# Values of the first attention as weights-stationary products, stored and turned by VectorE

## The chip, the core and the metric

The kernel runs on one core of one Trainium2 chip. The core has a matrix engine (TensorE, PE in the profile; its weight loads are listed as PEld), a vector engine (VectorE, DVE), an activation engine (ScalarE, ACT), a general engine (GpSimd, POOL), a queue engine (SyncE, SP) that issues nearly all transfers here, and 16 DMA engines. SBUF is the on-chip working memory with 128 partitions; PSUM is the accumulator memory that TensorE writes. The metric is device time in microseconds, the median of the runs.

## The reference

Two layers of gated cross attention and feed-forward over 8 batches of 128 tokens with 512 features. The change is in the first attention (32 heads of 128, 512-feature context):

```python
h_q = (x @ w_q.T).reshape(b, lq, H, DH)
h_k = (key_value_states @ w_k.T).reshape(b, lk, H, DH)
h_v = (key_value_states @ w_v.T).reshape(b, lk, H, DH)
score = jnp.einsum('bqhd,bkhd->bhqk', h_q, h_k) + position_bias[None]
score = softmax(where(mask, score, -inf))
attn = jnp.einsum('bhqk,bkhd->bqhd', score, h_v).reshape(b, lq, H * DH)
out = attn @ w_out.T
```

Then come a 4-bit-weight feed-forward, a second attention with one head of 512 features whose keys are also a projection of the context, and a feed-forward with routed low-rank parts. Everything is float32; products that need the precision are made from a high and a low part of each operand, three matmuls for one.

## The kernel before

**Three stages.** First the keys and queries of all heads are made and stored to DRAM (to about 300 us in the trace). Then come 64 attention units, about 7 us each (to about 770 us). The last stage runs the two feed-forwards and the second attention. A *unit* `u` is one head and one half of the batch (4 batches); a *pair* `p` is two heads, so four units; a *quad* `g` is four heads.

**Projections by seven products.** `seven` makes a 2 x 2 block product with seven block products instead of eight (Winograd's form): left blocks are the weights (`left_parts` builds the seven sums, `split` makes the high part on ScalarE and the low part on GpSimd or VectorE), right blocks are seven prepared sums of the context (`of_context`), kept in SBUF. It is a generator: one step, one block product. ScalarE copies four results out of PSUM, VectorE adds three.

For keys and queries (`tokens=None`) the weights are the stationary operand, and 512 columns of the context (4 batches x 128 tokens) move: the result has the head's features on the partitions and tokens along the row. One block product is 2 x 3 matmuls. For values (`tokens=jj`) it is the other way round: 128 tokens of the context are stationary and 256 weight columns (two heads) move, so that the result has tokens on the partitions, as the attention needs. One block product is 2 token blocks x 2 x 3 = 12 matmuls. `value_steps(g, jj)` makes a quad's values for half of each token range; `all_values` runs through eight quads, and a ninth that is not values but the second attention's keys (`wk1`). `quad_parts` makes the weight parts of the next quad while the present one is used. `make_values(n)` advances this work to step `n`; a unit asks for about 1.74 steps, 126 in all.

**A unit** (`unit(u)`): output projection for two batches of an earlier pair (`project_out`, six matmuls of 512 columns each and one VectorE add), value steps, `attend(u - 4)` (four matmuls of probabilities and values), then `add_masks(u)` on GpSimd and `scores(u)`: four score matmuls, add and maximum on VectorE, `transpose_probs(u - 3)` on VectorE, exponentials on ScalarE, reciprocal on VectorE, scaling on GpSimd.

**The probabilities' way round.** They have to be turned. VectorE transposes only blocks of 32 x 32, so blocks are moved first: `store_probs(u)` stores 256 KB to DRAM (`through`), `move_probs(u - 1)` reads them back by four transfers of 64 KB, 32 partitions each (`moved`), and `transpose_probs` turns them with one instruction over 128 x 512 elements.

**Order of the work.** The framework's scheduler orders the instructions of the units on each engine by its own estimate; in the first and last stage TensorE's order is that of the program. Each engine runs its instructions in order. `behind("name")` puts an instruction after the last one marked with that name on the same engine. SyncE runs its transfers in order too: per unit `through`, four `moved`, the fetches of one unit's queries and keys (`fetch`, two of 256 KB, three units ahead), and a load of weights (`load_wo`, `load_quad`). The transfers take turns at eight completion semaphores.

**Buffers.** `page` holds 14 buffers of 8 KB a partition (context parts, value weight parts, attention results), `v` 15 of 2 KB (values), `raw` 7. PSUM banks: `mm` 3 (value products and output projection), `sc` 2 (scores and one value product), `av` 3.

Of the kernel before, what the change touches and what calls it, by code (L numbers as in the profile page):

```python
# [17 lines left out]
P = 128  # L18
# [21 lines left out]
OUT_LAG = 6  # L40
FIRST = 6
SHORT = 12
QUAD = 4
AHEAD = 3
WARMING = 7


def pipeline(starts):
# [18 lines left out]
def kernel(  # L67
# [143 lines left out]
        put("P3", a12)  # L211
        yield

    def seven(name, left, right, kept, done, tokens=None):


        shape = [P, HALF * P] if tokens is None else [P, 2, N]

        def times(out, which, start, stop):
            w, t = left[which], right[RIGHT[which]]  # L220
            if tokens is None:
                terms = [
                    (
                        (w[:, 0, bass.ts(dc, P)], w[:, 1, bass.ts(dc, P)]),
                        (t[:, 0, dc, :], t[:, 1, dc, :]),
                    )
                    for dc in range(HK)
                ]
                product(out, terms, start, stop, skip_group_check=True)
                return  # L230
            for j in range(2):
                cols = bass.ts(2 * tokens + j, P)
                terms = [
                    (
                        (t[:, 0, dc, cols], t[:, 1, dc, cols]),
                        (w[:, 0, bass.ts(dc, N)], w[:, 1, bass.ts(dc, N)]),
                    )
                    for dc in range(HK)
                ]

                product(out[:, j, :], terms, start and j == 0, stop, skip_group_check=True)

        c1 = ptile(shape, "mm", f"c1_{name}")
        times(c1, "P1", True, False)
        c11 = kept(0, 0)
        mark("copy", nc.scalar.copy(c11, c1))
        yield
        c3 = ptile(shape, "av", f"c3_{name}")
        times(c3, "P5", True, False)
        yield  # L250
        times(c1, "P6", False, False)
        c12 = kept(0, 1)
        mark("copy", nc.scalar.copy(c12, c1))  # L253
        yield
        c2 = ptile(shape, "sc", f"c2_{name}")
        times(c2, "P2", True, True)
        mark("add", nc.vector.tensor_tensor(c11, c2, c11, ALU.add))
        done(0, 0, c11)
        yield
        times(c1, "P7", False, False)  # L260
        c22 = kept(1, 1)
        mark("copy", nc.scalar.copy(c22, c1))
        mark("add", nc.vector.tensor_tensor(c22, c3, c22, ALU.add))
        done(1, 1, c22)
        yield
        times(c1, "P4", False, True)
        c21 = kept(1, 0)
        mark("copy", nc.scalar.copy(c21, c1))
        done(1, 0, c21)
        yield  # L270
        times(c3, "P3", False, True)
        nc.vector.tensor_tensor(c12, c3, c12, ALU.add)
        done(0, 1, c12)
        yield

# [11 lines left out]

    def load_pair(kind, p):
        if p < NP:
            w = {"wk": wk, "wq": wq}[kind]  # L290
            for h in (2 * p, 2 * p + 1):
                load(f"{kind}_{h}", w[:, h])
# [22 lines left out]
                nc.vector.tensor_tensor(sums["P3"], sums["P2"], sums["P6"], ALU.subtract)  # L315
            yield

    def load_quad(g, rows=(0, 1)):

        for i in rows:  # L320
            for j in range(2):
                if g < H // 4:
                    load(f"wv{i}{j}_{g}", wv[:, 2 * g + i, 2 * j : 2 * j + 2])
                else:
                    src = wk1[:, 2 * j : 2 * j + 2, i * N : (i + 1) * N]
                    load(f"wv{i}{j}_{g}", src, (P, 2, N))

    quads = {}

    def quad_parts(g):  # L330

        blocks = [raws.pop(f"wv{i}{j}_{g}") for i in range(2) for j in range(2)]
        if g == H // 4:
            for n, t in enumerate(blocks):
                factor = fnw_p[:, n % 2 * 2 : n % 2 * 2 + 2].unsqueeze(2).to_broadcast([P, 2, N])
                nc.gpsimd.tensor_tensor(t, t, factor, ALU.mult)
            blocks = [t.rearrange("p a n -> p (a n)") for t in blocks]
        more = wide_row("raw", f"more_wv{g}")
        parts = quads[g] = {}
        pages = []  # L340

        def put(which, src):
            if len(parts) % 2 == 0:
                pages.append(page([P, 2, 2, D], f"wv{which}_{g}"))
            t = pages[-1][:, len(parts) % 2]
            by_vector = g < 2 and len(parts) % 2
            split(t[:, 0], t[:, 1], src, nc.vector if by_vector else nc.gpsimd)
            parts[which] = t

        yield from left_parts(*blocks, more, nc.vector if g < 2 else nc.gpsimd, put)  # L350

    wos = {}

# [296 lines left out]
            )  # L650
        nc.vector.tensor_reduce(anykey, mask_u8, AX.X, ALU.max)

    values_of, attns, probs = {}, {}, {}

    def value_steps(g, jj):

        def kept(n, half):
            return slot([P, 2, N], "v", f"v{n}{half}{jj}_{g}")  # L660

        def done(n, half, t):
            values_of[2 * g + n, half, jj] = t

        return seven(f"v{g}{jj}", quads[g], of_context, kept, done, jj)

    def where(u):

# [58 lines left out]

    def move_probs(u):
        moved = slot([P, NQ, HALF, Q32], "moved", f"moved_{u}")
        blocks = probs[u].rearrange("(i q) n f -> n q i f", q=Q32)  # L730
        for j in range(NQ):
            move = nc.sync.dma_start(
                out=moved[bass.ts(j, Q32)].rearrange("p i b k -> p i (b k)"), in_=blocks[j]
            )
        mark("moved", move)
        probs[u] = moved

    def transpose_probs(u):

        t = slot([P, HALF, P], "pT", f"pT_{u}")  # L740
        nc.vector.transpose(by_block(t), probs[u])
        probs[u] = t

    def attend(u):
        h, half = where(u)
        p, i = divmod(h, 2)
        pT = probs.pop(u)
# [4 lines left out]
        cols = bass.ts(i, P)  # L752
        av = ptile([P, HALF, P], "av", f"av_{u}")
        for b in range(HALF):
            v = values_of[p, half, b // 2][:, b % 2, :]
            nc.tensor.matmul(av[:, b, :], lhsT=v[:, cols], rhs=pT[:, b, :], start=True, stop=True)  # L756
        mark("a", nc.scalar.copy(ah, av))  # L757
        mark("al", nc.vector.tensor_tensor(al, av, wide(ah), ALU.subtract))  # L758

# [193 lines left out]
    def keys_and_queries():  # L953
        nonlocal left, sums, before
        for n, (kind, p) in enumerate(order[:-1]):
# [18 lines left out]
            for i, which in enumerate((now, now, before, now, before, now, now)):  # L974
                next(which, None)
                next(casts, None)
                if n == BEFORE // 2 and i == 3:

                    with later():
                        rows.append(next(of_rows))  # L980
                if i == 0:
                    if n + 2 < len(order):
                        load_pair("w" + order[n + 2][0][0], order[n + 2][1])
                    else:
                        load_quad(0)
            before = now
            with behind("add"):
                sums = sums_of(n + 2)
# [12 lines left out]
        parts = quad_parts(0)  # L1001
        for _ in range(2):
            next(parts)
        for u in range(FIRST):
            fetch(u)
# [8 lines left out]


    def all_values():
        for g in range(H // 4 + 1):
            more = g < H // 4
            if g == 0:
                load_quad(1)  # L1020
            yield from value_steps(g, 0)
            following = quad_parts(g + 1) if more else iter(())
            for n, _ in enumerate(value_steps(g, 1)):

                if n % 2 or n == 6:
                    next(following, None)
                    next(following, None)
                yield

    value_work = all_values()  # L1030
    made = 0
# [7 lines left out]
    def loads(u):  # L1039

        p, r = divmod(u, 4)

        n = {1: FIRST}.get(u, u + 3)
        if n > FIRST or u == 1:
            fetch(n)
        if u % 8 in (QUAD, QUAD + 1) and (u - QUAD) // 8 + 2 <= H // 4:
            load_quad((u - QUAD) // 8 + 2, (u % 8 - QUAD,))
# [142 lines left out]
    def keys(b):  # L1190
        half, j = divmod(b, HALF)
        k = work(b, "k", "v")
        for n in range(2):
            cols = bass.ts(n, N)
            with behind("al", "x"):
                nc.vector.scalar_tensor_tensor(
                    k[:, cols],
                    values_of[NP + n, half, j // 2][:, j % 2, :],
                    rcs[:, b : b + 1],
                    bk[:, cols],  # L1200
                    ALU.mult,
# [205 lines left out]
    def ending():  # L1407
# [7 lines left out]
        with behind("exp"):  # L1415
            split_wo(H - 1)
        move_probs(NU - 1)
        with behind("moved"):
            for i in range(2):
                w_ffn.extend(load_page(f"wf{i}", ffn_kept[i]))  # L1420
# [108 lines left out]
```

## Time and profile before

| | |
|---|---|
| median of 3 runs | 908.32 us (908.06 to 908.65) |
| the profiled execution, first to last instruction | 907.1 us |
| DMA traffic | 174.99 MB, mean 193 GB/s |
| issues of `moved` / `through` / `raw_wv` | 256 of 64 KB / 64 of 256 KB / 32 of 256 KB |
| median to landing | 3.0 us / 2.6 us / 4.9 us |
| granted TensorE clock | 1.000 |

The profile's page lists busy time of each engine, groups of instructions with their mean duration and the idle time before them, and DMA issues. Matmuls are pipelined, so the duration of one is longer than its share of the engine; the step from one start to the next is its price. A "stretch" row gives, for a part of the span: its limits and length, then busy us (and instructions) of PE, PEld, DVE, ACT and POOL, the granted clock, the busy share of the DMA engines, and GB/s. SyncE's rows are marked SPq: its time is issuing and waiting, none of it counted as busy.

### The profile page before, as it was taken

The numbers are of one execution on the slowest core, as the hardware profiler recorded it, in microseconds if no ns is written. First come the engines' busy times: TensorE is split into PE (matmuls) and PEld (weight loads), VectorE is DVE, ScalarE is ACT, GpSimd is POOL, SyncE is SP. The second block draws the span as 40 slices with busy tenths as digits, with TensorE's granted clock in tenths as the row PEclk, the third lists the DMA queues.
The fourth block names the chain that finished last, engine by engine and source line by source line (L and its number), as shares of the span: only waits on it lengthen the run. The fifth ranks groups of instructions, "written<-read, shape, count | busy, mean of one in ns | idle before, by whom it ended". The sixth has DMA issues, their size and how long they took to land.

```text
span 907.1 us, 16427 instructions
## 1 busy us (share of the span) xinstructions
PE 900.8 (99%) x5381; PEld 799.2 (88%) x5381; DVE 673.1 (74%) x1353; ACT 503.0 (55%) x1426; POOL 460.3 (51%) x513
## 2 busy tenths in 40 slices
PE   9999999999999999999999999999999999999998
PEld 7888888888888899999999999999999998888897
DVE  7888878789889866777677667666686877565587
ACT  6666555667555545545536445453454544588862
POOL 2355534114322436756747657583866844265441
PEclk9999999999999999999999999999999999999999
DMA  7755477889875956667574765766767566814001
GB/s 256 255 162 163 152 205 232 294 280 285 275 238 204 298 196 186 182 193 221 163 238 151 203 215 153 222 176 201 215 165 208 180 178 177 306 47 143 1 24 71
DMA packets 125223, 174.99 MB, mean 193 GB/s; under 512 B 17105, under 2 KB 54737, under 8 KB 124113
## 3 DMA queue, kind: packets, MB, share of 16 engines
q1 hardware_dynamic: 124992, 173.68, 61.5%
q8 instruction: 42, 0.69, 0.3%
q14 instruction: 45, 0.36, 0.1%
q10 hardware_dynamic: 144, 0.26, 0.1%
HBM read 109.86 MB, written 64.03 MB: 192 GB/s over the span
## 4 chain that ended last, share of the span: by engine, by line
PE 93%; DVE 3%; DMA 2%; ACT 1%; issue 0%; POOL 0%; SPq 0%; DVEq 0%; ACTq 0%; POOLq 0%
PE c_v L178 7%; PE c_v L179 6%; PE c_v L182 6%; PE pso L182 6%; PE pso L178 6%; PE pso L179 6%; PE sc L692 6%; PE av L756 6%; PE c_q L178 6%; PE c_q L179 6%; PE c_q L182 6%; PE c_k L178 4%; PE c_k L179 4%; PE c_k L182 4%; PE tph L1127 1%; DMA cxraw<-in_cxT_dram 1%
## 5 line engine op out<-in xcount | busy, mean ns | idle before, releaser
L709 ACT ACTIVATE s<-s,nm 128x128 f32<-128x128 f32 x256 | 99.8, 392 | 78.8 <-DVE nm L699 54.8
L777 DVE SCALAR_TENSOR_TENSOR x<-pso,tg,x 128x512 f32<-128x512 f32 x128 | 93.4, 741 | 52.2 <-PE pso L182 51.3
L717 POOL TENSOR_TENSOR s<-s,rs 128x512 f32<-128x512 f32 x64 | 66.7, 1042 | 111.1 <-DVE rs L715 63.2
L178 PE MATMUL pso<-wo_h,a 128*128 128x512 f32 x256 | 101.9, 411 | 0.0
L179 PE MATMUL pso<-wo_l,a 128*128 128x512 f32 x256 | 101.5, 397 | 0.0
L182 PE MATMUL pso<-wo_h,a 128*128 128x512 f32 x256 | 101.0, 395 | 0.1
L178 PE MATMUL c_v<-wvP,cxT 128*128 128x256 f32 x288 | 84.8, 294 | 0.2 <-ACT v L253 0.2
L182 PE MATMUL c_v<-wvP,cxT 128*128 128x256 f32 x288 | 81.4, 283 | 0.0
L179 PE MATMUL c_v<-wvP,cxT 128*128 128x256 f32 x288 | 81.4, 283 | 0.0
L757 ACT CAST a<-av 128x512 fp32r<-128x512 f32 x64 | 37.4, 584 | 74.4 <-PE av L756 74.0
L679 POOL TENSOR_TENSOR s<-mneg,bias 128x512 f32<-128x512 bf16 x64 | 75.9, 1186 | 0.1
L756 PE MATMUL av<-pT,v 128*128 128x128 f32 x512 | 71.2, 274 | 0.0
L756 PEld LDWEIGHTS av<-pT,v 128*128 128x128 f32 x512 | 67.1, 191 | 2.8
L692 PE MATMUL sc<-k,q 128*128 128x128 f32 x464 | 65.8, 274 | 0.0
L692 PEld LDWEIGHTS sc<-k,q 128*128 128x128 f32 x464 | 61.9, 191 | 3.2
L178 PE MATMUL c_v<-wvP,cxB 128*128 128x256 f32 x216 | 62.1, 289 | 0.0
L758 DVE TENSOR_TENSOR a<-av,a 128x512 fp32r<-128x512 f32 x64 | 43.4, 679 | 24.9 <-ACT a L757 24.5
L179 PE MATMUL c_v<-wvP,cxB 128*128 128x256 f32 x216 | 61.2, 283 | 0.0
L182 PE MATMUL c_v<-wvP,cxB 128*128 128x256 f32 x216 | 61.1, 283 | 0.0
L170 POOL TENSOR_TENSOR wo_l<-raw_wo,wo_h 128x512 fp32r<-128x512 f32 x32 | 41.4, 1293 | 33.8 <-ACT wo_h L169 33.8
L182 PEld LDWEIGHTS pso<-wo_h,a 128*128 128x128 f32 x256 | 48.2, 188 | 10.8 <-DVE a L758 1.3
L695 DVE TENSOR_TENSOR s<-sc,s 128x512 f32<-128x512 f32 x64 | 43.7, 683 | 17.1 <-PE sc L692 12.4
(277 smaller groups left out, 2808.4 us busy)
## 6 DMA issues: line engine op xcount, KB each, us to landing
keys<-keys SPq DMA_DIRECT2D x64, 256.0 KB, 3.5
queries<-queries SPq DMA_DIRECT2D x64, 256.0 KB, 3.5
through<-s SPq DMA_DIRECT2D x64, 256.0 KB, 2.6
moved<-through SPq DMA_DIRECT2D x256, 64.0 KB, 3.0
q<-queries SPq DMA_DIRECT2D x58, 256.0 KB, 3.8
k<-keys SPq DMA_DIRECT2D x58, 256.0 KB, 4.3
raw_wq<-in_wq_dram SPq DMA_DIRECT2D x32, 256.0 KB, 3.9
raw_wv<-in_wv_dram SPq DMA_DIRECT2D x32, 256.0 KB, 4.9
```

The source lines that it names most:

```text
L170: mark("low", (low_engine or nc.vector).tensor_tensor(low, src, wide(high), ALU.subtract))
L178: nc.tensor.matmul(out, lhsT=lh, rhs=rh, start=first, stop=False, **more)
L179: nc.tensor.matmul(out, lhsT=lh, rhs=rl, start=False, stop=False, **more)
L182: nc.tensor.matmul(out, lhsT=ll, rhs=rh, start=False, stop=last, **more),
L679: nc.gpsimd.tensor_tensor(s, mneg[:, half], bias.unsqueeze(2).to_broadcast([P, NQ, HALF, Q32]), ALU.add)
L692: nc.tensor.matmul(ps[:, j, :], lhsT=q[:, cols], rhs=k[:, cols], start=True, stop=True)
L695: nc.vector.tensor_tensor(s, by_block(ps), s, ALU.add)
L709: e = nc.scalar.activation(one, one, AF.Exp, bias=nm[:, j : j + 1], accum_out=sm[:, j : j + 1])
L717: mark(f"norm{u}", nc.gpsimd.tensor_tensor(s, s, factors, ALU.mult))
L756: nc.tensor.matmul(av[:, b, :], lhsT=v[:, cols], rhs=pT[:, b, :], start=True, stop=True)
L758: mark("al", nc.vector.tensor_tensor(al, av, wide(ah), ALU.subtract))
L777: "x", nc.vector.scalar_tensor_tensor(xs[b], ps, factor, xs[b], ALU.mult, ALU.add, **out)
```

## The change

Values are made as keys are: a pair's weights are stationary, 512 columns of context move, one block product is six matmuls of 512 columns. The result has features on the partitions, so it is stored to DRAM (ordered by 32-token blocks while it is copied out of PSUM, through `view`), read back by four transfers of 32 partitions each, and turned by one VectorE transpose a unit, right after the probabilities' own. The weight parts are made a pair at a time (seven of 256 columns), the first four pairs half on VectorE. The ninth quad, the second attention's keys, is made as before, under new names.

```diff
-    def seven(name, left, right, kept, done, tokens=None):
+    def seven(name, left, right, kept, done, tokens=None, view=lambda t: t):
...
-        mark("copy", nc.scalar.copy(c11, c1))
+        mark("copy", nc.scalar.copy(c11, view(c1)))
...
-        mark("add", nc.vector.tensor_tensor(c11, c2, c11, ALU.add))
+        mark("add", nc.vector.tensor_tensor(c11, view(c2), c11, ALU.add))
...
+    def value_weights(p):
+
+        rows = [raws.pop(f"wv_{h}") for h in (2 * p, 2 * p + 1)]
+        more = slot([P, HK, P], "raw", f"more_wv{p}")
+        a11, a12, a21, a22 = (t[:, :, bass.ts(i, P)] for i in range(2) for t in rows)
+        parts = value_parts[p] = {}
+        pages = []
+        engine = nc.vector if p < BY_VECTOR else nc.gpsimd
+
+        def put(which, src):
+            n = len(parts)
+            if n % 4 == 0:
+                pages.append(page([P, 4, 2, HK, P], f"wv{which}_{p}"))
+            t = pages[-1][:, n % 4]
+            split(t[:, 0], t[:, 1], src, nc.vector if p < BY_VECTOR and n % 2 else nc.gpsimd)
+            parts[which] = t.rearrange("p a dc n -> p a (dc n)")
+
+        yield from left_parts(a11, a12, a21, a22, more, engine, put)
...
-    def value_steps(g, jj):
+    def value_steps(p):
+
+        def kept(i, half):
+            return slot([P, NQ, HALF, Q32], "v", f"v{i}{half}_{p}")
+
+        def done(i, half, t):
+            stored_v = dram.tile([P, NQ, HALF * Q32], F32, tag="values", name=f"values_{p}{i}{half}", bufs=VALUES)
+            with behind("load"):
+                nc.sync.dma_start(out=stored_v, in_=t.rearrange("p n b k -> p n (b k)"))
+            values_of[4 * p + 2 * half + i] = stored_v
+
+        def view(t):
+            return by_block(t.rearrange("p (b k) -> p b k", b=HALF))
+
+        return seven(f"v{p}", value_parts[p], of_context, kept, done, view=view)
...
+    def turn(name, src, moved):
+
+        blocks = src.rearrange("(i q) n f -> n q i f", q=Q32)
+        for j in range(NQ):
+            move = nc.sync.dma_start(
+                out=moved[bass.ts(j, Q32)].rearrange("p i b k -> p i (b k)"), in_=blocks[j]
+            )
+        mark(name, move)
+
+    def move_values(u):
+        if 0 <= u < NU:
+            t = slot([P, NQ, HALF, Q32], "v", f"vmoved_{u}")
+            turn("values", values_of[u], t)
+            values_of[u] = t
+
+    def transpose_values(u):
+        t = slot([P, HALF, P], "v", f"vT_{u}")
+        nc.vector.transpose(by_block(t), values_of[u])
+        values_of[u] = t
...
     def transpose_probs(u):
...
         probs[u] = t
+        transpose_values(u)
...
-            v = values_of[p, half, b // 2][:, b % 2, :]
-            nc.tensor.matmul(av[:, b, :], lhsT=v[:, cols], rhs=pT[:, b, :], start=True, stop=True)
+            nc.tensor.matmul(
+                av[:, b, :], lhsT=v[:, b, :], rhs=pT[:, b, :], start=True, stop=True
+            )
...
     def all_values():
+        load_pair("wv", 2)
+        for p in range(NP):
+            following = value_weights(p + 1) if p + 1 < NP else last_weights()
+            for _ in value_steps(p):
+                next(following, None)
                 yield
+            run(following)
+        for jj in range(2):
+            yield from last_steps(jj)
...
         p, r = divmod(u, 4)
 
+        move_values(u - 2)
         n = {1: FIRST}.get(u, u + 3)
...
         move_probs(NU - 1)
+        move_values(NU - 1)
         with behind("moved"):
```

The new constants are `BY_VECTOR = 4` (pairs whose weight parts are half VectorE's) and `VALUES = 14` (buffers in DRAM for stored values). `loads(u + 1)` is called in unit `u`, so `move_values(u - 2)` there reads the values of unit `u - 1`, after the probabilities of the same unit.

More of the change, by code (lines that the diff above doesn't have):

```diff
@@ L42 @@
 SHORT = 12
-QUAD = 4
 AHEAD = 3
 WARMING = 7
+BY_VECTOR = 4
+VALUES = 14
 def pipeline(starts):
@@ L252, in seven @@
         c12 = kept(0, 1)
-        mark("copy", nc.scalar.copy(c12, c1))
+        mark("copy", nc.scalar.copy(c12, view(c1)))
         yield
@@ L261, in seven @@
         c22 = kept(1, 1)
-        mark("copy", nc.scalar.copy(c22, c1))
-        mark("add", nc.vector.tensor_tensor(c22, c3, c22, ALU.add))
+        mark("copy", nc.scalar.copy(c22, view(c1)))
+        mark("add", nc.vector.tensor_tensor(c22, view(c3), c22, ALU.add))
         done(1, 1, c22)
@@ L267, in seven @@
         c21 = kept(1, 0)
-        mark("copy", nc.scalar.copy(c21, c1))
+        mark("copy", nc.scalar.copy(c21, view(c1)))
         done(1, 0, c21)
@@ L271, in seven @@
         times(c3, "P3", False, True)
-        nc.vector.tensor_tensor(c12, c3, c12, ALU.add)
+        nc.vector.tensor_tensor(c12, view(c3), c12, ALU.add)
         done(0, 1, c12)
@@ L289, in load_pair @@
         if p < NP:
+            if kind == "wv":
+                for i in range(2):
+                    load(f"wv_{2 * p + i}", wv[:, p, 2 * i : 2 * i + 2], (P, 2, N))
+                return
             w = {"wk": wk, "wq": wq}[kind]
@@ L316, in pair_parts, with load_last, last_weights @@
             yield
-    def load_quad(g, rows=(0, 1)):
-        for i in rows:
-            for j in range(2):
[L322 to L339, printed above, removed]
+    value_parts = {}
+    def value_weights(p):
[13 more added lines that the diff above has]
+        yield from left_parts(a11, a12, a21, a22, more, engine, put)
+    def load_last():
+        for i in range(2):
+            for j in range(2):
+                src = wk1[:, 2 * j : 2 * j + 2, i * N : (i + 1) * N]
+                load(f"wk1{i}{j}", src, (P, 2, N))
+    def last_weights():
+        blocks = [raws.pop(f"wk1{i}{j}") for i in range(2) for j in range(2)]
+        for n, t in enumerate(blocks):
+            factor = fnw_p[:, n % 2 * 2 : n % 2 * 2 + 2].unsqueeze(2).to_broadcast([P, 2, N])
+            nc.gpsimd.tensor_tensor(t, t, factor, ALU.mult)
+        blocks = [t.rearrange("p a n -> p (a n)") for t in blocks]
+        more = wide_row("raw", "more_wk1")
+        parts = value_parts[NP] = {}
         pages = []
@@ L343, in put @@
             if len(parts) % 2 == 0:
-                pages.append(page([P, 2, 2, D], f"wv{which}_{g}"))
+                pages.append(page([P, 2, 2, D], f"wk1{which}"))
             t = pages[-1][:, len(parts) % 2]
-            by_vector = g < 2 and len(parts) % 2
-            split(t[:, 0], t[:, 1], src, nc.vector if by_vector else nc.gpsimd)
+            split(t[:, 0], t[:, 1], src, nc.gpsimd)
             parts[which] = t
-        yield from left_parts(*blocks, more, nc.vector if g < 2 else nc.gpsimd, put)
+        yield from left_parts(*blocks, more, nc.gpsimd, put)
     wos = {}
@@ L651, in prep_mask, with last_steps @@
         nc.vector.tensor_reduce(anykey, mask_u8, AX.X, ALU.max)
-    values_of, attns, probs = {}, {}, {}
-    def value_steps(g, jj):
+    values_of, last_of, attns, probs = {}, {}, {}, {}
+    def value_steps(p):
[9 more added lines that the diff above has]
+        return seven(f"v{p}", value_parts[p], of_context, kept, done, view=view)
+    def last_steps(jj):
         def kept(n, half):
-            return slot([P, 2, N], "v", f"v{n}{half}{jj}_{g}")
+            return slot([P, 2, N], "v", f"k1{n}{half}{jj}")
         def done(n, half, t):
-            values_of[2 * g + n, half, jj] = t
-        return seven(f"v{g}{jj}", quads[g], of_context, kept, done, jj)
+            last_of[n, half, jj] = t
+        return seven(f"k1{jj}", value_parts[NP], of_context, kept, done, jj)
+    def turn(name, src, moved):
[14 more added lines that the diff above has]
+        values_of[u] = t
     def where(u):
@@ L729, in move_probs @@
         moved = slot([P, NQ, HALF, Q32], "moved", f"moved_{u}")
[L730 to L735, printed above, removed]
+        turn("moved", probs[u], moved)
         probs[u] = moved
@@ L746, in attend @@
         p, i = divmod(h, 2)
-        pT = probs.pop(u)
+        pT, v = probs.pop(u), values_of.pop(u)
         if i == 0:
@@ L751, in attend @@
         ah, al = a[:, 0], a[:, 1]
-        cols = bass.ts(i, P)
         av = ptile([P, HALF, P], "av", f"av_{u}")
         for b in range(HALF):
-            v = values_of[p, half, b // 2][:, b % 2, :]
-            nc.tensor.matmul(av[:, b, :], lhsT=v[:, cols], rhs=pT[:, b, :], start=True, stop=True)
+            nc.tensor.matmul(
+                av[:, b, :], lhsT=v[:, b, :], rhs=pT[:, b, :], start=True, stop=True
+            )
         mark("a", nc.scalar.copy(ah, av))
@@ L984, in keys_and_queries @@
                     else:
-                        load_quad(0)
+                        load_pair("wv", 0)
+                        load_pair("wv", 1)
             before = now
@@ L1000, in keys_and_queries @@
                     next(extra, None)
-        parts = quad_parts(0)
-        for _ in range(2):
+        parts = value_weights(0)
+        for _ in range(3):
             next(parts)
@@ L1016, in all_values @@
     def all_values():
[L1017 to L1027, printed above, removed]
+        load_pair("wv", 2)
[3 more added lines that the diff above has]
+                next(following, None)
                 yield
+            run(following)
+        for jj in range(2):
+            yield from last_steps(jj)
     value_work = all_values()
@@ L1045, in loads @@
             fetch(n)
-        if u % 8 in (QUAD, QUAD + 1) and (u - QUAD) // 8 + 2 <= H // 4:
-            load_quad((u - QUAD) // 8 + 2, (u % 8 - QUAD,))
+        q = {2: 3}.get(u, p + 3 if p and r == 0 else NP + 1)
+        if q < NP:
+            load_pair("wv", q)
+        elif q == NP:
+            load_last()
         if r == 1:
@@ L1197, in keys @@
                     k[:, cols],
-                    values_of[NP + n, half, j // 2][:, j % 2, :],
+                    last_of[n, half, j // 2][:, j % 2, :],
                     rcs[:, b : b + 1],
```

## The prediction

> **What bounds the kernel now.** I read four views in this order: the page's busy times, the stretches, the PE timeline, and SyncE's queue.
>
> ```profile
> span 907.1 us, 16427 instructions
> PE 900.8 (99%) x5381; PEld 799.2 (88%) x5381; DVE 673.1 (74%) x1353; ACT 503.0 (55%) x1426; POOL 460.3 (51%) x513
> ```
>
> The stretch of the attention units, where all the value products lie but the first and last few (PE, PEld, DVE, ACT, POOL busy, granted clock, DMA share, GB/s):
>
> ```profile
> 350.00:750.00 400.00, 400.00 (x2785) 371.14 (x2784) 281.53 (x498) 197.47 (x652) 261.82 (x226) 1.00 0.66 194
> ```
>
> PE has no idle time there, at full clock. No other engine passes 70%, and the DMA engines are 66% busy. The 58 stores of probabilities in that stretch make 58 units, 6.90 us each. So a shorter PE stream shortens the kernel, as long as nothing else reaches 6.9 us a unit.
>
> Busy means overlap, so the price of a matmul is read from start to start (start, duration, name):
>
> ```profile
> 201.20 0.39 PE L179 MATMUL c_q<-xqT,wqP 128*128 128x512 f32 x1
> 201.43 0.39 PE L182 MATMUL c_q<-xqT,wqP 128*128 128x512 f32 x1
> 201.65 0.39 PE L178 MATMUL c_q<-xqB,wqP 128*128 128x512 f32 x1
> ```
>
> ```profile
> 503.14 0.28 PE L178 MATMUL c_v<-wvP,cxB 128*128 128x256 f32 x1
> 503.26 0.28 PE L179 MATMUL c_v<-wvP,cxB 128*128 128x256 f32 x1
> 503.38 0.28 PE L182 MATMUL c_v<-wvP,cxB 128*128 128x256 f32 x1
> ```
>
> 512 columns cost 0.2265 us (median step of the query products), 256 columns 0.120 us.
>
> SyncE issues nearly every transfer. Its queue in a dense stretch, the stretch's shares, and the waits in that queue (total, times, longest):
>
> ```profile
> 508.10 0.38 SPq L725 DMA_DIRECT2D through<-s  x1
> 508.58 1.92 SPq L732 DMA_DIRECT2D moved<-through  x4
> 510.94 0.34 SPq L615 DMA_DIRECT2D q<-queries  x1
> 511.75 0.34 SPq L615 DMA_DIRECT2D k<-keys  x1
> 512.52 0.33 SPq L285 DMA_DIRECT2D raw_wo<-in_wo_dram  x1
> 513.26 0.32 SPq L725 DMA_DIRECT2D through<-s  x1
> ```
>
> ```profile
> 508.10:513.30 5.20, 5.20 (x35) 4.69 (x34) 4.53 (x9) 3.11 (x14) 1.67 (x2) 1.00 0.94 251
> ```
>
> ```profile
> SPq L725 <- POOL s L717: 112.0, 38, 5.8
> SPq L564 <- DVE keys L272: 29.3, 11, 3.0
> SPq L615 <- DMA k<-keys: 8.1, 15, 1.0
> ```
>
> Eight transfers took 5.2 us here, at 94% of the DMA engines: when SyncE has work it is already short of room. The program uses eight completion semaphores in turn, so an issue waits for the transfer issued eight before; the last of these rows is that wait. Today its spare time is the 112 us spent waiting for the next normalized probabilities.
>
> **The change part by part.**
>
> *Matmuls.* A quad of heads took 2 x 7 products x 2 tokens x 2 x 3 = 168 matmuls of 256 columns; eight quads, 1344. A pair now takes 7 x 2 x 3 = 42 of 512; sixteen pairs, 672. The multiply work is equal; the gain is 672 x (2 x 0.120 - 0.2265) = 9.1 us, all on the path. The last quad (second layer's keys) stays.
>
> The Trainium skill ("TensorE: Matmul & The Clock Gate", Back-to-back issue gap) speaks against even this: it gives 262 and 518 cycles, 109 and 216 ns at the full clock, so a pair of halves would lose only 2.5 ns and the change would save 672 x 2.5 ns = 1.7 us. The rows above show 13.5 ns, and they decide.
>
> *Turning.* 64 more VectorE transposes at the row of the existing ones: 64 x 0.702 = 44.9 us. VectorE goes in the stretch from 281.5 to about 281.5 + 58 x 0.70 = 322 us of 400, 81%. It was at 92% (45.98 of 50 us) at 250 to 300 us with PE full, so I cost this at nothing beside PE. Without cover it is the 44.9 us.
>
> *Splitting the weights.* 112 splits of 256 columns replace 56 of 512. ScalarE: 112 x 0.409 - 56 x 0.620 = +11 us. GpSimd, by these rows:
>
> ```profile
> L170 POOL TENSOR_TENSOR wvP<-raw_wv,wvP 128x512 fp32r<-128x512 f32 x41 | 54.0, 1329 | 2.8 <-ACT wvP L169 2.7
> L170 POOL TENSOR_TENSOR wkP<-raw_wk,wkP 128x256 fp32r<-128x256 f32 x33 | 27.6, 847 | 42.2 <-ACT wkP L169 40.2 <-DMA em_i<-in_expert_map_dram 1.9
> L741 DVE STREAM_TRANSPOSE pT<-moved 128x512 f32<-128x512 f32 x64 | 44.8, 702 | 5.0 <-DMA moved<-through 4.9
> ```
>
> 100 x 0.847 - 50 x 1.329 = +18 us, and the sums 48 x 0.85 - 24 x 1.30 = +10 us: GpSimd rises from 65% to about 72%. Both are hidden. In the built order most parts still stand some four units ahead of their product; the tightest (pair 9) have about two. Copies and adds of the products keep their number; the reordered PSUM read costs nothing (score add at L695, same access, 683 ns; plain add L257, 685).
>
> *Transfers.* Each unit adds one 256 KB store (like `through`) and four 64 KB reads (like `moved`), all on SyncE: 320 issues. In the stretch there were 470, so 8.1 a unit become 13.1. Three accounts for one unit:
> - DMA engines: 0.656 x 6.90 = 4.53 us now. The store is 128 packets of 2 KB at 109 ns, the reads 512 packets of 512 B at 28.7 ns, over 16 engines: +0.87 +0.92 = 6.3 us.
> - Eight transfers in flight: mean landing is 3.81 us over those issues. (8.1 x 3.81 + 3.55 + 4 x 3.44) / 8 = 6.0 us at today's landing times; 13.1 x 4.7 / 8 = 7.7 us if all landed like the weight loads (median 4.7).
> - Issue itself: the four `moved` above take 0.48 us each, 13.1 x 0.48 = 6.3 us. In the 12 unbroken runs inside the units (14 issues or more, none over 1.3 us after the one before), the step is 0.50 to 0.63 us, median 0.56: 7.3 us.
>
> PE needs 6.90 - 9.1/64 = 6.76 us. The bounds are therefore 6.3 us (hidden, the 9.1 us stay) and 7.3 us (64 x 0.4 = 28 us more than now). The new mix has more small transfers than the dense runs, so less data an issue; engines at 95% would give 6.3/0.95/13.1 = 0.51 us. Between 0.51 and 0.56 I take 0.535: 13.1 x 0.535 = 7.01 us.
>
> The Trainium skill ("DMA: Bandwidth & Descriptors", Anatomy of one DMA) puts a fixed 2.0 us on a transfer, on the GpSimd path, plus bytes over 436 GB/s: 2.15 us for 64 KB. Its estimate for eight in flight would be under 4 us a unit and the queue no limit; the 64 KB reads here land in 3.4 us on average.
>
> *Waits added.* A value store waits in SyncE's queue for VectorE's add or ScalarE's copy; behind it stand the next `through`, the `moved` reads and the fetches of q and k. The like stores of keys and queries (L564) cost 1 to 3 us of queue each when SyncE came early. The value reads come right after the probabilities' reads, so land about 4 x 0.48 = 1.9 us behind them; the value transpose waits for them in VectorE's queue, ahead of the output adds that free PE's banks. In 17 of 64 units the probabilities landed less than 1.5 us before their transpose. The built order answers by placing most attends five units behind their scores, not four. The ending gains four issues and three transposes, about 2 us, beside other products.
>
> **Sum.** 64 x (7.01 - 6.90) = +7.0 us: span 914.1. The median stands 1.2 us above the profiled span (908.3 against 907.1), so 915.3, rounded to 915.
>
> **The rivals.**
> 1. *SyncE and the DMA engines keep up; PE stays the bound.* For it: the stage at 200 to 250 us ran at 89% DMA share with PE full, and loads are issued three units ahead or more. Against it: that stage has large transfers and few issues. Time 908.3 - 9.1 = 899; with a few us lost at start and end, up to 906. It decides if an issue costs under 0.515 us. Chance 0.37.
> 2. *No change:* losses of 7 to 11 us eat the gain. Chance 0.06.
> 3. *VectorE blocked by late values.* Slower too: in the 17 tight units the added 1.9 + 0.7 us stops the output adds and so PE, 17 x 2.6 = 44 us less 9, if the extra unit of lag doesn't absorb it: 943. Against it is just that lag. Chance 0.09.
> 4. *The forecast,* 911 to 937: the transfer queue sets the unit. Chance 0.48.
>
> That the products themselves don't come faster is nearly excluded: the query products are the same instruction stream.
>
> **How the numbers follow.** Faster 0.37, slower 0.48 + 0.09 = 0.57, same (within 0.2%, about what a measurement of this kernel can tell) 0.06. The likeliest case's own range is 911 to 937 (0.53 to 0.56 us an issue). Both signs are likely, so the range reaches to the full gain, 898, and up to 937.
>
> **What would show it.** Right: SyncE issues nearly without pause from 350 to 750 us, its wait for L717's work shrinks well below 112 us, DMA share near 0.9, units near 7.0 us, and PE idle for the first time there, before attends or output products, some 15 us in all. Rival 1: PE still 400 of 400. Rival 3: idle time before the value transposes, released by their reads. The steps of the products should be 0.227 us in every case; if they are near 0.24, the gain falls.

## The result and the profile after

The changed kernel takes 960.77 us (median of 4 runs, 957.91 to 964.40); the kernel before took 908.35 us beside it (908.06 to 908.65). The ratio is 1.0581, with a 95% interval of 1.0565 to 1.0596: 52 us slower. The profiled execution spans 957.7 us, 50.6 us more than before.

Four marks place the loss: the first and the last maximum over scores (the `nm` instruction on VectorE, one a unit), the start and the end.

| us | before | after |
|---|---|---|
| start to first maximum | 319.5 | 322.3 |
| first to last maximum, 63 units | 435.0 (6.90 each) | 482.8 (7.66 each) |
| last maximum to the end | 152.6 | 152.7 |

So 48 of the 51 us were lost where the units run. The page of after (span and engines; then the chain of waits by engine; three groups with their busy time, mean and the idle time before them; two rows of transfer issues with the size of one and the median time to landing):

```profile
span 957.7 us, 15785 instructions
...
PE 906.8 (95%) x4709; PEld 767.3 (80%) x4709; DVE 703.6 (73%) x1431; ACT 508.6 (53%) x1482; POOL 472.0 (49%) x587
...
PE 60%; DMA 21%; SPq 6%; DVE 5%; issue 3%; POOL 3%; ACT 2%; DVEq 0%; POOLq 0%; ACTq 0%
...
L746 PE MATMUL sc<-k,q 128*128 128x128 f32 x464 | 70.4, 280 | 32.9 <-DMA k<-keys 27.1
...
L790 DVE STREAM_TRANSPOSE pT<-moved 128x512 f32<-128x512 f32 x64 | 45.3, 708 | 70.2 <-DMA moved<-through 58.7
...
moved<-through SPq DMA_DIRECT2D x256, 64.0 KB, 4.1
vmoved<-values SPq DMA_DIRECT2D x256, 64.0 KB, 2.8
```

The page of the kernel before has for the chain and for the scores:

```profile
PE 93%; DVE 3%; DMA 2%; ACT 1%; issue 0%; POOL 0%; SPq 0%; DVEq 0%; ACTq 0%; POOLq 0%
...
L692 PE MATMUL sc<-k,q 128*128 128x128 f32 x464 | 65.8, 274 | 0.0
```

PE falls from 99% to 95% of a longer span, and transfers with their queue now hold 27% of the chain that ended last, where they held 2%. What PE waits for is above all the keys of a unit, read back from DRAM for its scores: 27.1 us. VectorE waits 58.7 us for probabilities before it can turn them, where it waited 4.9 us before. No row of this size names the new value reads.

SyncE's queue in after (start, duration, line, transfer), one unit of it:

```profile
434.68 0.38 SPq L683 DMA_DIRECT2D values<-v  x1
435.15 0.38 SPq L779 DMA_DIRECT2D through<-s  x1
435.58 2.77 SPq L705 DMA_DIRECT2D moved<-through  x4
438.39 1.92 SPq L705 DMA_DIRECT2D vmoved<-values  x4
440.41 0.38 SPq L634 DMA_DIRECT2D q<-queries  x1
440.83 1.28 SPq L634 DMA_DIRECT2D k<-keys  x1
442.15 0.43 SPq L286 DMA_DIRECT2D raw_wo<-in_wo_dram  x1
442.69 0.38 SPq L779 DMA_DIRECT2D through<-s  x1
```

From one `through` to the next it takes 7.5 us, and nothing in between is a pause: each line starts within 0.1 us of the end of the one before it. Most issues take 0.3 to 0.5 us. One of the four `moved` here takes 1.22 us and the `k` 1.28; both began after the transfer eight before them had landed, so why they are long the trace does not show. Waits for a landing stand ahead of an issue, as a gap; those of that queue between 350 and 750 us (total, times, longest):

```profile
SPq L705 <- DMA through<-s: 12.0, 33, 1.2
SPq L705 <- DMA k<-keys: 9.2, 22, 0.9
SPq L705 <- DMA raw_wv<-in_wv_dram: 7.5, 21, 0.9
SPq L779 <- POOL s L771: 7.4, 9, 1.4
```

The spare time is gone: in this stretch SyncE waited 104.6 us for normalized probabilities before, and 7.4 us now. In these 400 us it issued 677 transfers against 470, so 0.59 us went on each: by the queue's rows 304 us in the issues themselves (0.45 each; 55 of them took over 0.55 us), some 34 us in small gaps (0.05 each) and 62 us in longer ones (0.09 each). Of the waits, 50 us are put down to earlier transfers.

The `k` fetch above is one that comes too late. PE's timeline of after at that place, and stretches of after (limits and length, busy us of PE, PEld, DVE, ACT and POOL, granted clock, DMA share, GB/s):

```profile
446.01 1.77 PE L746 MATMUL sc<-k,q 128*128 128x128 f32 x8 [2.18 <-DMA k<-keys]
```

```profile
350.00:750.00 400.00, 361.43 (x1952) 306.24 (x1950) 273.86 (x498) 180.81 (x625) 241.03 (x267) 0.99 0.81 240
...
354.00:356.00 2.00, 0.00 (x0) 0.00 (x0) 1.21 (x2) 1.15 (x4) 1.90 (x3) 0.54 0.76 160
356.00:358.00 2.00, 1.78 (x4) 1.49 (x5) 0.00 (x0) 0.17 (x1) 0.51 (x1) 0.50 0.85 290
...
446.00:448.00 2.00, 1.99 (x9) 1.91 (x10) 0.00 (x0) 1.30 (x3) 2.00 (x3) 0.58 0.86 252
448.00:450.00 2.00, 2.00 (x7) 1.57 (x6) 1.36 (x3) 0.00 (x0) 1.46 (x3) 0.57 0.68 211
```

The scores waited 2.18 us, and PE is idle for 38.6 of the 400 us where it was idle for none. 26.6 us of that were for `k`. Around two of its pauses (this one, and one of 4.32 us at 352, ahead of a value product, for a ScalarE copy) the granted clock was also down to half, for 3.4 and 6.8 us: some 4 us of work. Between the two marks PE is idle for 43 us in 36 pauses. Counted from start to start, the steps with a pause in them are 49 us longer than the usual ones, 6 more than the idle time, since the last matmul before a pause is shown for longer than its step. With the 4 us of the clock that makes 53. As the shorter products saved 4.3 us between the marks (`products_turns`, below), 52 are to be explained, so this covers the loss within what such a count can tell.

### The profile page after: what moved, and what is told of

Read it like the earlier page. It is cut to its first block, busy times and chain, and to the rows that moved or that the text cites. A ratio compares the mean times of both kernels' runs of the same rounds, so it can differ in the third digit from the quotient of the medians.

```text
span 957.7 us, 15785 instructions
## 1 busy us (share of the span) xinstructions
PE 906.8 (95%) x4709; PEld 767.3 (80%) x4709; DVE 703.6 (73%) x1431; ACT 508.6 (53%) x1482; POOL 472.0 (49%) x587
## 4 chain that ended last, share of the span: by engine, by line
PE 60%; DMA 21%; SPq 6%; DVE 5%; issue 3%; POOL 3%; ACT 2%; DVEq 0%; POOLq 0%; ACTq 0%
DMA k<-keys 7%; DMA through<-s 5%; PE c_q L179 5%; PE c_q L180 5%; PE c_q L183 5%; PE c_k L179 5%; PE c_k L180 5%; PE c_k L183 5%; DMA moved<-through 5%; SPq L705 3%; PE sc L746 3%; PE pso L179 2%; PE c_v L179 2%; PE pso L183 2%; PE pso L180 2%
## 5 line engine op out<-in xcount | busy, mean ns | idle before, releaser
L763 ACT ACTIVATE s<-s,nm 128x128 f32<-128x128 f32 x256 | 99.8, 391 | 98.9 <-DVE nm L753 49.3
L179 PE MATMUL pso<-wo_h,a 128*128 128x512 f32 x256 | 107.1, 423 | 2.6 <-DVE x L827 2.4
L183 PE MATMUL pso<-wo_h,a 128*128 128x512 f32 x256 | 101.6, 400 | 0.0
L746 PE MATMUL sc<-k,q 128*128 128x128 f32 x464 | 70.4, 280 | 32.9 <-DMA k<-keys 27.1
L746 PEld LDWEIGHTS sc<-k,q 128*128 128x128 f32 x464 | 65.3, 192 | 45.3 <-DVE s L749 17.6
L790 DVE STREAM_TRANSPOSE pT<-moved 128x512 f32<-128x512 f32 x64 | 45.3, 708 | 70.2 <-DMA moved<-through 58.7
L804 PEld LDWEIGHTS av<-pT,vT 128*128 128x128 f32 x512 | 67.3, 191 | 10.5 <-issue 3.5
L804 PE MATMUL av<-pT,vT 128*128 128x128 f32 x512 | 69.8, 275 | 4.4 <-DVE vT L718 4.4
L171 POOL TENSOR_TENSOR wvP<-raw_wv,wvP 128x256 fp32r<-128x256 f32 x72 | 53.1, 756 | 19.9 <-ACT wvP L170 12.3
L179 PEld LDWEIGHTS pso<-wo_h,a 128*128 128x128 f32 x256 | 48.7, 190 | 12.3 <-DVE x L827 4.7
L179 PE MATMUL c_v<-cxT,wvP 128*128 128x512 f32 x128 | 53.4, 417 | 4.3 <-ACT v L254 4.3
L183 PEld LDWEIGHTS pso<-wo_h,a 128*128 128x128 f32 x256 | 48.3, 189 | 10.6 <-DVE a L808 0.9
L180 PEld LDWEIGHTS pso<-wo_l,a 128*128 128x128 f32 x256 | 48.7, 190 | 7.0
L180 PE MATMUL c_v<-cxT,wvP 128*128 128x512 f32 x128 | 50.5, 395 | 0.0
```

Source lines behind the costliest of these rows:

```text
L171: mark("low", (low_engine or nc.vector).tensor_tensor(low, src, wide(high), ALU.subtract))
L179: nc.tensor.matmul(out, lhsT=lh, rhs=rh, start=first, stop=False, **more)
L180: nc.tensor.matmul(out, lhsT=lh, rhs=rl, start=False, stop=False, **more)
L183: nc.tensor.matmul(out, lhsT=ll, rhs=rh, start=False, stop=last, **more),
L746: nc.tensor.matmul(ps[:, j, :], lhsT=q[:, cols], rhs=k[:, cols], start=True, stop=True)
L763: e = nc.scalar.activation(one, one, AF.Exp, bias=nm[:, j : j + 1], accum_out=sm[:, j : j + 1])
```

## The experiments

All times are medians; the kernel before took 908.3 to 908.6 us on the same chips. "Unit" is first to last maximum over 63; "issues" are all transfers issued per unit and "each" the time for one of them, both between 350 and 750 us; "idle" is 400 us less PE's busy time there, and the last column is the busy share of the DMA engines there.

| kernel | us | ratio to before | unit | issues | each | idle | DMA |
|---|---|---|---|---|---|---|---|
| before | 908.35 | | 6.90 | 8.1 | 0.85 | 0.0 | 0.66 |
| products_turns | 902.31 | 0.9932 (0.9912 to 0.9952) | 6.84 | 8.1 | 0.85 | 0.5 | 0.66 |
| merged | 912.40 | 1.0049 (1.0032 to 1.0065) | 6.97 | 9.1 | 0.77 | 6.4 | 0.94 |
| one_read | 919.85 | 1.0125 (1.0105 to 1.0145) | 7.04 | 10.1 | 0.70 | 8.8 | 0.85 |
| small_writes | 946.83 | 1.0426 (1.0398 to 1.0453) | 7.51 | 13.1 | 0.57 | 21.1 | 0.66 |
| after | 960.77 | 1.0581 (1.0565 to 1.0596) | 7.66 | 13.0 | 0.59 | 38.6 | 0.81 |

Where transfers are too many, "each" is what an issue costs; where they are few, it holds spare time. Read downwards, the time mostly follows the number of issues, not the bytes: `small_writes` moves about as little as the kernel before, `merged` as much as after. The bytes are not free either: `small_writes` and after have as many issues and differ by 14 us. What the table does not separate is an issue's own time from its wait for one of the eight semaphores, as both come with every issue.

### The products without the transfers

`products_alone` takes the values' round trip out of the changed kernel, and the turn with it:

```diff
         def done(i, half, t):
-            stored_v = dram.tile([P, NQ, HALF * Q32], F32, tag="values", ...
...
-            values_of[4 * p + 2 * half + i] = stored_v
+            values_of[4 * p + 2 * half + i] = t
...
         if 0 <= u < NU:
-            t = slot([P, NQ, HALF, Q32], "v", f"vmoved_{u}")
-            turn("values", values_of[u], t)
-            values_of[u] = t
+            pass
 
     def transpose_values(u):
-        t = slot([P, HALF, P], "v", f"vT_{u}")
-        nc.vector.transpose(by_block(t), values_of[u])
-        values_of[u] = t
+        values_of[u] = values_of[u].rearrange("p n b k -> p (n b k)").rearrange("p (b k) -> p b k", b=HALF)
```

> The changed kernel without the store, the four reads and the turn of the values: the attention takes the product tile as it is, so the values are left unturned. Transfer-queue theory: the new products are worth their 9 us and the split weights cost nothing, TensorE is busy 400 of 400 us in the units again; 897 to 902 us. Rival (512 columns bring nothing in the units, or GpSimd's smaller pieces hold TensorE back): 907 us or more, with TensorE idle before value products.

It took 904.12 us (903.66 to 904.25, 4 runs), ratio 0.9951 (0.9934 to 0.9967): a gain, but 4.3 us and not 9, between the two expectations.

`products_turns` has the first two of these edits and keeps `transpose_values`, so VectorE turns each value tile straight from the product:

> As products_alone, with VectorE's 64 added transposes (of the product tile straight from SBUF, no store and no reads, so blocks stay where they are and the output is not the reference's). Transfer-queue theory: VectorE's 45 us are hidden, within 2 us of products_alone. Rival (VectorE's added work holds TensorE back): 5 us or more above it.

It took 902.31 us (902.11 to 902.50). The stretch of `products_turns`, in the columns used above:

```profile
350.00:750.00 400.00, 399.55 (x2261) 347.52 (x2260) 315.37 (x565) 204.39 (x703) 274.79 (x294) 1.00 0.66 195
```

PE is full at full clock with VectorE at 79% and GpSimd at 69%: 64 more transposes and the smaller weight parts cost PE nothing here. It even ended 1.8 us before `products_alone`. This is what the change would bring if the values needed no transfers: 6 us. Its values are turned by blocks only, so it is a measurement and no kernel to use.

`no_turn` is the opposite half: the changed kernel with all its transfers, and only the last edit above, no VectorE turn of the values.

> The changed kernel with store and reads of the values, but without VectorE's transpose of them (the attention takes the tile as read). Transfer-queue theory: the transfers alone cost it, 950 to 960 us, SyncE issues without pause. Rival (VectorE blocked by its added transposes and their waits): back to 900 to 915 us.

It took 967.89 us (965.62 to 970.16), ratio 1.0654 (1.0623 to 1.0684), 8 us over the expectation and not faster than after at all. Its stretch, and VectorE's longest wait in the whole run:

```profile
350.00:750.00 400.00, 364.25 (x1916) 307.17 (x1917) 240.10 (x441) 179.00 (x618) 238.01 (x264) 0.97 0.80 235
```

```profile
DVE pT L788 <- DMA moved<-through: 95.5, 41, 6.4
```

VectorE is less busy than in any other kernel here (240 of 400 us) and waits 95.5 us for probabilities. The VectorE rival falls; the loss is in the transfers. Why it is 7 us slower than after is open; its granted clock is lower, 0.97 in the stretch against 0.99.

### How many, or how large

`one_read` reads a unit's values back by one transfer of 256 KB instead of four of 64 KB:

```diff
-            turn("values", values_of[u], t)
+            nc.sync.dma_start(out=t.rearrange("p n b k -> p n (b k)"), in_=values_of[u])
```

> The changed kernel with the values read back by one transfer of 256 KB a unit instead of four of 64 KB (same bytes, rows of 2 KB; the 32-row blocks are not regrouped, so the output is not the reference's). Issues a unit 13.1 to 10.1. Theory that the number of transfers sets the unit (issue and eight in flight, 0.57 to 0.59 us each): 10.1 x 0.59 = 6.0 us, TensorE becomes the bound again, 900 to 908 us. Rival (bytes and the DMA engines set it): 940 us or more.

It took 919.85 us (919.54 to 920.15), between the two expectations. Three issues fewer a unit give back 41 of the 52 us with the bytes unchanged. This read also has rows of 2 KB instead of 512 bytes, so the number of issues is not alone in it; `merged`, below, keeps the short rows. 17.5 us remain over `products_turns`, for two transfers of 256 KB a unit; how much of that rest is issues and how much bytes this run does not say.

`small_writes` asks the question without any of the change: the kernel before, with five writes of 16 KB a unit, of constant rows, to a place in DRAM that nobody reads.

```diff
+    spare = [dram.tile([P, P], F32, tag=f"spare{n}", name=f"spare{n}", bufs=1) for n in range(2)]
+
     def loads(u):
...
+        for j in range(NQ + 1):
+            rows = bass.ts(j % NQ, Q32)
+            nc.sync.dma_start(out=spare[j // NQ][rows], in_=ident[rows])
```

> The kernel before with five added writes of 16 KB a unit (32 rows of a constant to a spare DRAM buffer), issued by SyncE just ahead of the fetches of q and k: 13.1 issues a unit as in the changed kernel, with 5% more bytes instead of 39%. Theory that SyncE's time per issue sets the unit: 13.1 x 0.50 us (issue and the gap after it, without waits for landing) = 6.5 us and more with the rest of its waits, so slower than before by 5 to 40 us. Rival (bytes on the DMA engines set it): 906 to 911 us, as before.

It took 946.83 us (944.95 to 948.71): 38 us more than the kernel before, the upper end of what was expected, and the rival that only bytes count falls. SyncE's queue in `small_writes`, and its waits between 350 and 750 us:

```profile
530.46 1.93 SPq L732 DMA_DIRECT2D moved<-through  x4
532.83 2.85 SPq L1047 DMA_DIRECT2D spare<-ident  x5
535.78 0.37 SPq L615 DMA_DIRECT2D q<-queries  x1
```

```profile
SPq L1047 <- DMA k<-keys: 15.8, 29, 1.7
SPq L1047 <- DMA raw_wo<-in_wo_dram: 13.3, 25, 1.2
SPq L1047 <- DMA through<-s: 12.5, 32, 1.2
```

Five writes hold the queue for 2.85 us, 0.57 us each, more than the `moved` reads of four times the size (0.48). Their issues alone take 0.30 to 0.42 us here; the rest is gaps ahead of them, for they stand behind larger transfers: an issue waits until the transfer eight before it has landed, and the small ones come too fast after `k`, `raw_wo` and `through`. The DMA engines stay at 66%. So five more issues a unit alone cost 38 us, where the change lost 52 (58 against `products_turns`, which has its faster products).

### Other engines issue the reads

`reads_act` and `reads_pool` let ScalarE or GpSimd issue the four value reads:

```diff
-    def turn(name, src, moved):
+    def turn(name, src, moved, queue=nc.sync):
...
-            move = nc.sync.dma_start(
+            move = queue.dma_start(
...
-            turn("values", values_of[u], t)
+            turn("values", values_of[u], t, nc.scalar)
```

(`nc.gpsimd` in the other.)

> The changed kernel with the four reads of the values issued by ScalarE instead of SyncE; all else equal, and the eight completion semaphores are still shared. Theory that SyncE's time per issue sets the unit: SyncE has 9.1 issues left, 905 to 925 us (ScalarE has four more issues, about 2 us a unit, of its 3.4 us idle). Rival (eight transfers in flight set it): 945 us or more.

> The changed kernel with the four reads of the values issued by GpSimd, which have completion semaphores of their own. If SyncE's issues and the semaphores were all, 900 to 915 us; GpSimd is busy about 4.7 us of 6.8 in a unit, so if one issue costs it more than 0.5 us, GpSimd becomes the bound and the time stays above 930 us. Bytes theory: 940 us or more either way.

`reads_act` took 947.58 us (947.07 to 948.10), ratio 1.0434 (1.0413 to 1.0455). `reads_pool` took 974.64 us (974.59 to 974.69), ratio 1.0732 (1.0711 to 1.0753). Two of ScalarE's waits in `reads_act`:

```profile
ACT s L763 <- DMA vmoved<-values: 42.3, 11, 6.5
...
ACT wvP L170 <- DMA vmoved<-values: 33.4, 8, 8.0
```

The exponentials (L763) now stand behind the value reads on ScalarE. SyncE was relieved of its issues and not of its waits: in the 400 us it waited 154 us for earlier transfers, where in after it was 50. The mean number of transfers in flight, by my count over the trace, rose from 6.6 to 7.3: the reads that ScalarE issues carry the same eight completion semaphores as SyncE's transfers, so an issue still waits for the eighth before it, now also on an engine that had work to do. That was the rival written for this run, and it is the nearer. The Trainium skill ("DMA: Bandwidth & Descriptors", Issuing engines are not separate DMA queues) says that issuing from several engines saves only the issuing engine's own time; with 13 of the 52 us given back, the 947.58 us agree.

In `reads_pool` the group of these reads (busy, mean of one) and the stretch:

```profile
L705 POOL DMA_DIRECT2D vmoved<-values x256 | 140.8, 557 | 3.5 <-issue 3.5
```

```profile
350.00:750.00 400.00, 364.51 (x1931) 304.77 (x1930) 282.70 (x499) 179.50 (x622) 342.64 (x460) 0.98 0.82 237
```

One issue keeps GpSimd busy for 557 ns, 140.8 us in all, and GpSimd, which also scales the probabilities, goes to 86% of the stretch. That this sets the time is not shown: PE's idle time in the stretch (35.5 us) is spread over waits for value transposes, fetched keys and output adds, and the granted clock fell to half five times up to 800 us, for 31 us in all. From first to last maximum the run is even 9 us shorter than after (474.0 against 482.8); the part behind is 24 us longer. The bytes theory, which also allowed 940 us or more, is not tested by this run.

### The same bytes in fewer issues

`merged` keeps the whole change, but stores a unit's probabilities and values in one DRAM buffer, so that four reads of 128 KB bring both:

```diff
-    "page": 14, "v": 15, ...
+    "page": 14, "v": 13, ...
...
+            both = dram.tile([2, P, NQ, HALF * Q32], F32, tag="values", name=f"values_{p}{i}{half}", bufs=VALUES)
...
+                nc.sync.dma_start(out=both[1], in_=t.rearrange("p n b k -> p n (b k)"))
+            values_of[4 * p + 2 * half + i] = both
...
-        blocks = src.rearrange("(i q) n f -> n q i f", q=Q32)
+        blocks = src.rearrange("w (i q) n f -> n q (w i) f", q=Q32)
...
+        both = values_of[u]
+        through = both[0]
...
+        probs[u] = both
...
-        moved = slot([P, NQ, HALF, Q32], "moved", f"moved_{u}")
+        moved = slot([P, 2, NQ, HALF, Q32], "moved", f"moved_{u}")
...
-        nc.vector.transpose(by_block(t), probs[u])
+        values_of[u] = probs[u][:, 1]
+        nc.vector.transpose(by_block(t), probs[u][:, 0])
```

> The changed kernel with probabilities and values of a unit in one DRAM buffer, so that four reads of 128 KB bring both (buffers for values in SBUF 13 instead of 15, two for reads of double size). 9.1 issues a unit, bytes and 512-byte rows as in the changed kernel. Issue theory: below one_read (919.9), 900 to 918 us. Bytes theory: 935 us or more.

It took 912.40 us (912.16 to 912.92, 4 runs): 48 of the 52 us are back with the bytes unchanged, as the issue theory expected. The page's issue row of `merged`, and its stretches:

```profile
moved<-values SPq DMA_DIRECT2D x256, 128.0 KB, 4.8
```

```profile
350.00:750.00 400.00, 393.59 (x2202) 340.11 (x2201) 305.92 (x552) 197.87 (x684) 268.98 (x290) 1.00 0.94 266
...
440.00:470.00 30.00, 28.13 (x157) 24.00 (x156) 23.87 (x43) 14.77 (x52) 23.30 (x25) 1.00 1.03 289
```

A read of twice the size lands 0.7 us later by the median, and 9.1 issues a unit fit. The DMA engines are now 94% busy, and full at 440 to 470 us. PE's 6.4 us of idle time in the 400 are as much as the products gain. They stand ahead of output products (2.3 us, for VectorE's adds), attends (2.2, for value transposes) and a weight's low part from GpSimd (1.9); none of them names a transfer, so that the DMA load is the limit that is left is not shown.

`half` tries a lower load: it makes values in this way for every second quad only, and the others as before:

```diff
+    def new_pair(p):
+        return p // 2 % 2 == 1
...
+        if new_pair(u // 4):
+            values_of[u] = both[:, 1]
+            transpose_values(u)
```

> merged for every second quad of heads only (pairs 2, 3, 6, 7, 10, 11, 14, 15 by the new products with values and probabilities read together; the other pairs and their transfers as in the kernel before; 13 buffers for values). 8.6 issues a unit on average and half the added bytes, DMA share about 0.80 by the mean of 0.66 and 0.94. Theory that the change lost to SyncE's issues, transfers in flight and DMA load, each near its limit: below the limits TensorE sets the time again, half of the gain of products_turns, 908.4 - 3.0 = 905.4 us (904 to 907). Rival (any added transfer in the units costs TensorE time, or the long stretch of mixed forms costs order): 909 to 915 us.

It took 910.04 us (908.60 to 913.23 in 11 runs), ratio 1.0024 (1.0014 to 1.0035): a miss, 3 us over the expected range and inside the rival's. Its stretches, and PE's timeline behind them:

```profile
350.00:750.00 400.00, 399.79 (x2494) 357.98 (x2493) 296.72 (x532) 199.88 (x677) 271.61 (x262) 1.00 0.81 234
750.00:800.00 50.00, 47.05 (x276) 39.92 (x275) 32.10 (x67) 25.37 (x57) 12.93 (x21) 1.00 0.69 230
```

```profile
761.71 0.50 PE L179 MATMUL pso<-wo_h,a 128*128 128x512 f32 x1 [1.99 <-DVE x L883]
```

The transfers fit (DMA share 0.81, PE idle for 0.2 of 400 us), yet the last maximum comes 2.6 us later than before, and the part behind it is 3 us shorter: work moved, and little was saved. Where the units end PE waits for VectorE's output adds, 2 us in the line shown. Half of the products' gain was 3 us; that these pauses are what ate it was not tried. The profiled execution is also the fastest of the 11 (908.60 us), so what made the others up to 4.6 us slower is not in this trace. No version that keeps the values' way round, whole or for half of them, beats the kernel before.

## Why the prediction failed, point by point

**The matmuls.** The median step was right: 512 columns of a value product go in 0.227 to 0.228 us in all kernels with the new products. The sum was too large: `products_turns` gained 6.0 us where 9.1 stood. Its units are 4.3 us shorter in all, the part behind the last maximum 3.5 us (28.2 against 31.7 to the feed-forward's first product), and the start is 1.5 us longer, before its first maximum. The medians were the wrong price. Summed from start to start, the 1344 steps of the kernel before take 165.3 us, the 672 of `products_turns` 160.7 and those of `products_alone` 159.3: 4.6 and 6.0 us less, a mean of 0.123 us for the old step and 0.239 or 0.237 for the new. Some 60 steps in each kernel are about 0.08 us longer than the median, and with 672 steps 0.01 us a step is already 6.7 us.

**The turns and the weight parts** were rightly costed at nothing. VectorE came to 315 of 400 us in `products_turns` where 322 was worked out, GpSimd to 69% where 72% was, and PE was idle for 0.5 of the 400 us.

**The transfers are the step that failed**: "Between 0.51 and 0.56 I take 0.535: 13.1 x 0.535 = 7.01 us." The count was right (13.0), the price was 0.59, so the unit was 7.66 us: 64 x (7.66 - 6.90) = 49 us, where the forecast had 7. Of the three accounts, that of the DMA engines came out as forecast (6.3 us; 0.81 x 7.66 = 6.2). The eight in flight, at the landing times of after (3.92 us on average), make 13.0 x 3.92 / 8 = 6.4 us. The issues alone, 13.0 x 0.45, make 5.9. Each is below the 6.84 us that PE needs in `products_turns`, and the unit still took 7.66, because in one queue they add: 0.45 of issuing, 0.05 of small gaps and 0.09 of longer ones make the 0.59, and with next to no spare time in the queue a wait is not made up for. I took a midpoint between a perfect packing and the median of the bursts in the kernel before. So the mechanism was right and the price of an issue was too low. A burst is what a queue looks like when it is full, and its median of 0.56 was no upper bound. After's steady value is inside the spread of those bursts (0.50 to 0.63). (The upper bound's "64 x 0.4 = 28" is 64 x 0.44, from 13.1 x 0.56.)

**The likeliest case's range** of 911 to 937 rested on 0.53 to 0.56 and failed for the same reason. The overall range, whose upper end was 937, failed with it.

**Where PE waits** was wrong. With the queue at 7 us a unit I expected PE idle for some 15 us, ahead of attends or output products. That it was 38.6 us in 400 follows from the unit's 7.66 us; but 31 of them stand ahead of the scores, 26.6 for the fetched keys. The fetches stand last in each unit's turn, and that they lose their lead there when the queue falls behind is my reading; no run moved them. The 4 us that the lower clock cost were in no term.

**The waits added.** The value transposes do not hold VectorE: they waited 7.9 us for their reads in the whole run, while the probabilities' transposes waited 58.7 us for theirs. Rival 3 had the wrong reads; `no_turn` leaves it no room. The ending took 152.7 us where `products_turns` took 149.0: 3.7 us more, where 2 were forecast for the added work.

**The rivals.** Rival 1 (SyncE keeps up, 899 to 906) named its own condition, under 0.515 us an issue, and that was not met; `products_turns`, where the added transfers are gone, lies inside its range at 902.31. The direction came from rival 4's mechanism, and of its signs SyncE's queue without pause and the shrunken wait (104.6 to 7.4 us in the stretch) were there. The DMA share was to be near 0.9 and is 0.81, since the unit grew more than the traffic.

## What to carry to other kernels

Before adding transfers to a queue that one engine issues in order, count the issues per unit of work and price them by what the queue does when it is already full, at the slower bursts and not at the best ones; here 0.57 to 0.59 us with the waits, whether the added issues moved 16 KB or 64 and 256 KB. If the sum comes near the unit, merge transfers before anything else: the same bytes in 9 issues a unit instead of 13 gave back 48 of 52 us, while issuing from another engine gave back 13 or made it worse. A layout change on the matrix engine is worth only what its way round through DRAM leaves of it.

## What the runs showed of the hardware

- Small transfers are not quick ones. In after, reads of 64 KB land in 2.8 us (`vmoved`) and 4.1 us (`moved`) by the median, stores of 256 KB in 4.7 us (`through`); the 16 KB writes of `small_writes` needed 2.2 us, and 0.57 us of the queue each in the row shown, waits included.
- A transfer issued by GpSimd kept it busy for 557 ns. A run of reads issued by ScalarE left ScalarE idle for up to 8.0 us, while one after the other waited until an earlier transfer had landed (`reads_act`).
- In after, the granted clock fell to 0.50 during a pause of PE of 4.32 us, and again right after one of 2.18 us; matmuls of 512 columns then went in steps of 0.42 us instead of 0.227. The Trainium skill ("TensorE: Matmul & The Clock Gate", HAM oscillation — how this bites in real kernels) names pauses above about 3.4 us. The second one here was shorter, and the measurement decides. The length of a pause alone does not tell, though: four others of 2.12 to 2.22 us in after went without a drop.
